# A two-layer hybrid transformer in fp32 on one core: the gate and the decay of the linear attention, and the ends of the first workspace layer, are computed by other engines and in another order

## The chip, the cores and the metric

The kernel runs on one core of a Trainium2 chip. The core has five engines that run side by side, each with its own queue of instructions in a fixed order: TensorE (PE, matrix products and transposes; PEld is its loading of weights), VectorE (DVE), ScalarE (ACT), GpSimd (POOL) and SyncE (SP), which here starts all the transfers. Engines wait for each other through semaphores. The metric is the device time of one execution in microseconds (us); lower is better.

## The reference

The input x has 4 sequences of 512 rows of 256 numbers, all fp32. Eight blocks follow one another, each added to x: latent attention with 16 heads, a small feed-forward block, cosine-similarity attention, the feed-forward block again, gated linear attention, a workspace layer, attention with LoRA adapters, and a workspace layer again. The gated linear attention and the end of a workspace round are what the change touches:

```python
# gated linear attention, for each sequence, 16 heads (dk = 8, dv = 16)
gk = jax.nn.log_sigmoid(x @ Wgk1 @ Wgk2 + bgk2) / 16
S  = S * jnp.exp(gt)[..., None] + kt[..., None] * vt[..., None, :]     # step over t
ot = jnp.einsum('bhk,bhkv->bhv', qt, S)
o  = o * jax.lax.rsqrt(jnp.mean(o * o, axis=-1, keepdims=True) + EPS) * norm_w
o  = o * (g * jax.nn.sigmoid(g))              # g = x @ Wg
out = o.reshape(b, t, vd) @ Wo

# workspace layer, two rounds; 16 slots gather from x, then x reads the slots
ws = _rms(ws + written, norm_post_w)
x_b = ctx @ out_proj_w.T + out_proj_b         # ctx: attention of x over the slots
x  = _rms(x + x_b, norm_post_w)
# after the two rounds the layer's result is added to the residual x
```

In the LoRA attention each sequence has its own adapted weights, W + A B, chosen by an index of the sequence.

## The kernel before

Rows lie on the 128 partitions: a sequence is 4 tiles of 128 rows (NI = 4), and the 256 columns are 2 halves (NC = 2). x stays on the chip for the whole kernel, in one buffer per sequence, and is loaded once and stored once. The stages follow one another: latent attention (0 to about 700 us, with the feed-forward steps of finished sequences woven in), cosine attention (to 1411), gated linear attention (to about 1605), the first workspace layer (to about 1732), LoRA attention (from 1750), the second workspace layer (to about 2204), and the store.

The order of work on PE is the order of the program text, since the whole emission runs inside a manual schedule for PE. Later stages reach into earlier ones by generators: a table called `woven` gives points (n, k) of a stage's loop at which the next step of another generator is emitted. The order on DVE, ACT, POOL and SP is chosen by the language's scheduler, which plays the program through a timeline of its own and takes what comes first in it; a block under `high_priority` is taken earlier. Buffers come from pools with a fixed number of copies, and an instruction that writes a buffer waits until its last reader is done.

**Gated linear attention.** `gla_load` and `gla_fold` (L753 to L769) load and prepare the weights; among them is the bias column `bg`, read by ACT. `gla_stage` has `prepare(b, part)` for a sequence's projections: "norm" is the layernorm of x into `xn`, with the last step, x times 1/deviation plus an offset, on ACT (L178 makes the offset on DVE, L180 is the ACT step); "turned" transposes `xn` on PE (L195) and copies the result to `own_xt` on ACT (L196); part 1 is the decay (L815 to L821), parts 2 to 4 are v, q and k. `run` then goes through 4 sequences and 4 blocks of each; a block has two pairs of `states`: PE spreads v over partitions (L857), DVE multiplies with k in PSUM (L858) and scans over time, twice 512 columns (L861), POOL multiplies with q (L866), and PE sums (L876, `reads`). `gate` (L838 to L845) makes the gate of a sequence: a Sigmoid on ACT from PSUM, a reload of ACT's table for logarithm and exponential, and a DVE product with the same PSUM tile. `output` (L892 to L907) normalises by heads: a scaling on DVE (L899), ACT (L900, L901), four operations on POOL (L903 to L906; for the last sequence on DVE), and a DVE product (L907).

The decay of a sequence is exp of log-sigmoid over 16, with log-sigmoid(z) = min(z, 0) − ln(1 + exp(−|z|)). Before, ACT makes z (L815), |z| (L816), exp (L817), ln (L818), DVE takes min and subtracts (L819), ACT takes the exponential (L821).

A generator `first` folds the gated stage's weights and prepares sequence 0 at the points (15, 0), (15, 1), (15, 3), (16, 1) and (16, 2) of the cosine stage, and, as its last step at (16, 3), the layernorm of sequence 1.

**Workspace layer.** `ws_load` (L962) loads its weights and scales some of them on DVE (L968, L970, L971). In `ws`, `layernorm` writes the normalised x to `xf` on ACT; `turned` transposes it. Each of two rounds picks and gathers rows for the slots, and then goes over the sequences, a few steps apart: `attend`, `turn`, and `read` (L1224 to L1243): PE multiplies, DVE adds to `xf` (L1228), ACT squares for the mean (L1231), DVE and ACT make 1/root (L142 to L148, L143 and L144), DVE multiplies by it and by the weight `post` (four times L1234), and in round 1 DVE adds the result to the residual x (L1243).

**LoRA attention.** `lora_steps` (L1325) makes for a sequence the layernorm (with the last step on DVE, L185), two adapted weights (`adapted`: a DVE scaling L1347, two pairs of PE products, a DVE addition L1352), the transposes (L1362) with an ACT copy (L1363), and projections with rotary products on DVE (L1375) and sums on POOL. For the first sequence all of it is emitted after the workspace layer's last instruction. `keep(n)` (L217) emits n products of the identity with a mask into a spare PSUM buffer.

## Time and profile before

| | us |
|---|---|
| median of 3 runs (2207.63 to 2209.11) | 2208.92 |
| the profiled execution | 2209.9 |
| its span, first to last instruction | 2208.2 |
| PE busy in the span | 1985.9 |
| DVE busy | 1301.7 |
| ACT busy | 764.2 |
| POOL busy | 562.1 |
| mean granted TensorE clock (1 is full) | 0.953 |

The time of an execution is longer than its span by what lies around the first and the last instruction, here 1.7 us. In a line of a timeline the first number is the start from the span's beginning, the second the duration, then the engine, the source line, the operation, the written and the read buffers, and the shapes (partitions by columns); "x8" is a run of eight like instructions, and the bracket gives the time that the engine stood idle just before and what ended it.

### The profile page before, as it was taken

Reading aid. Unit: us, or ns where it says so; the run is one execution under the profiler, and the core shown is the slowest. Engines: PE = TensorE matmul, PEld = TensorE weight load, DVE = VectorE, ACT = ScalarE, POOL = GpSimd, SP = SyncE. Lnnn points to the kernel's source line nnn. Section 1 sums busy time; section 2 is a strip of 40 time slices with the busy share of each in tenths; the row PEclk is TensorE's granted clock in tenths of the full one; section 3 lists DMA queues with packets and bytes.
Section 4 is the critical chain, followed back from the end, with each engine's and each line's share of the span. In section 5 each row is a group of like instructions: output and inputs, shape, how many; then the busy total and the mean of one; then the engine's idle time right before and its main releaser. Section 6 shows DMA issues by size and latency. Waiting matters only on the chain.

```text
span 2208.2 us, 25496 instructions
## 1 busy us (share of the span) xinstructions
PE 1985.9 (90%) x9348; PEld 1061.1 (48%) x9348; DVE 1301.7 (59%) x3225; ACT 764.2 (35%) x1696; POOL 562.1 (25%) x489
## 2 busy tenths in 40 slices
PE   6999999998899999999999999787787679998885
PEld 4556555564444544544455454433254434444454
DVE  4565655656446435644753554599945766667455
ACT  2433434434223222322232242243134224334442
POOL 2333333433212122112211222065510012222100
PEclk9999999999899999999999999898789889999898
DMA  4020000000000000000000000100000000000001
GB/s 173 1 89 1 1 1 1 1 1 1 20 0 0 1 0 0 1 0 0 1 1 1 0 0 1 45 0 0 1 24 1 0 1 1 1 1 1 1 1 39
DMA packets 19838, 22.88 MB, mean 10 GB/s; under 512 B 4832, under 2 KB 17664, under 8 KB 19328
## 3 DMA queue, kind: packets, MB, share of 16 engines
...
q8 instruction: 74, 1.21, 0.2%
...
## 4 chain that ended last, share of the span: by engine, by line
PE 60%; DVE 18%; issue 11%; ACT 5%; POOL 4%; DMA 1%; SPq 0%; POOLq 0%; DVEq 0%; ACTq 0%
PE ps_two L215 26%; PE ps_acc L215 10%; PE ps_two L366 6%; PE ps_two L1410 4%; PE ps_acc L405 3%; PE ps_two L393 3%; DVE ps_two L233 3%; POOL e L661 2%; DVE gs L861 2%; PE ps_two L1452 2%; DVE ln_st L166 1%; PE ps_acc L1196 1%; DVE ps_st L858 1%; PE ps_two L628 1%; DMA x<-in_x 1%
## 5 line engine op out<-in xcount | busy, mean ns | idle before, releaser
L661 POOL TENSOR_TENSOR e<-e 128x1024 f32<-128x1024 f32 x64 | 150.6, 2353 | 623.0 <-ACT e L653 604.7
L233 DVE CUSTOM_DVE_ANT_0 ps_two<-ps_two,mask 128x128 f32<-128x128 f32 (+3 forms) x512 | 249.7, 502 | 80.2 <-PE ps_two L366 43.6
L653 ACT ACTIVATE e<-ps_two 128x1024 f32<-128x1024 f32 x128 | 130.7, 1022 | 351.1 <-PE ps_two L215 350.9
L215 PE MATMUL ps_acc<-e,cv 128*128 128x512 f32 x512 | 235.0, 602 | 1.4 <-DVE cot L659 0.9
L215 PE MATMUL ps_two<-cq,ckt 128*128 128x512 f32 x512 | 232.1, 596 | 3.0 <-DVE cq L630 3.0
L378 POOL TENSOR_TENSOR prob<-prob,psum_row 128x256 f32<-128x256 f32 (+3 forms) x128 | 159.4, 1254 | 289.2 <-DVE psum_row L377 283.0
L373 ACT ACTIVATE prob<-ps_two,nmax 128x128 f32<-128x128 f32 (+3 forms) x256 | 132.3, 525 | 148.4 <-DVE nmax L233 137.6
L215 PEld LDWEIGHTS ps_acc<-e,cv 128*128 128x128 f32 x512 | 93.4, 190 | 138.6 <-issue 115.8
L215 PEld LDWEIGHTS ps_two<-cq,ckt 128*128 128x128 f32 x512 | 97.2, 191 | 117.9 <-issue 115.5
L215 PE MATMUL ps_two<-own_xt,s 128*128 128x512 f32 x200 | 108.0, 672 | 18.4 <-DVE prt L129 10.6
L215 PE MATMUL ps_two<-own_xt,s16a 128*128 128x512 f32 x256 | 114.9, 593 | 0.1
L215 PE MATMUL ps_two<-s16b,cot 128*128 128x256 f32 x512 | 113.1, 379 | 0.0
L366 PE MATMUL ps_two<-kvt,qx 64*128 64x384 f32 (+3 forms) x512 | 104.5, 485 | 8.8 <-ACT qx L354 4.7
L1441 ACT ACTIVATE lo_ex<-ps_two 128x1024 f32<-128x1024 f32 (+3 forms) x128 | 85.4, 704 | 73.8 <-PE ps_two L1410 69.5
L393 PE MATMUL ps_two<-ident,prob 128*128 128x128 f32 x640 | 96.1, 282 | 15.5 <-POOL prob L378 5.8
L393 PEld LDWEIGHTS ps_two<-ident,prob 128*128 128x128 f32 x640 | 72.1, 143 | 76.7 <-issue 49.1
L215 PEld LDWEIGHTS ps_two<-s16b,cot 128*128 128x128 f32 x512 | 97.3, 190 | 20.1 <-issue 7.7
L1442 POOL TENSOR_SCALAR_AFFINE_SELECT lo_ex<-lo_ex 128x256 f32<-128x256 f32 x128 | 51.5, 407 | 196.5 <-ACT lo_ex L1441 195.3
L662 DVE TENSOR_TENSOR es<-e 128x512 f32<-128x512 f32 x64 | 43.9, 686 | 95.1 <-POOL e L661 94.0
L366 PE MATMUL ps_two<-kpe,qy 64*128 64x384 f32 (+3 forms) x512 | 91.5, 434 | 1.1 <-POOL qy L300 1.1
L1410 PE MATMUL ps_two<-lo_qm,lo_t 32*128 32x128 f32 (+3 forms) x512 | 78.0, 488 | 10.0 <-ACT lo_ex L1441 5.3
L405 PE MATMUL ps_acc<-prt,kv 128*64 128x256 f32 (+3 forms) x512 | 80.1, 457 | 3.4 <-DVE prt L129 3.4
...
## 6 DMA issues: line engine op xcount, KB each, us to landing
...
```

Of the source, the lines that this page charges most:

```text
L215: self.nc.tensor.matmul(out, lhsT=l, rhs=r, start=k == 0, stop=k == n - 1)
L233: self.nc.vector.tensor_tensor_reduce(out=sc[:, :n], in0=sc[:, :n], in1=self.mask[:, T - n :], scale=-1.0, scalar=3.0e38, op0=ALU.add, op1 ...
L366: nc.tensor.matmul(sc[:, k, :n], lhsT=q[r, rows], rhs=key[r, :n], start=first, stop=not first)
L373: nc.scalar.activation(pr[:, k, :n], sc[:, k, :n], AF.Exp, bias=nm[:, k : k + 1], scale=-1.0, accum_out=sm[:, k : k + 1],)
L378: nc.gpsimd.tensor_tensor(pr[:, :, :n], pr[:, :, :n], sm.unsqueeze(2).to_broadcast([P, 2, n]), op=ALU.mult)
L393: nc.tensor.transpose(pt[:, k, keys], pr[:, k, keys], self.ident)
L405: nc.tensor.matmul(po[k * R : (k + 1) * R, j * P :], lhsT=s.kv[:, j, 0, :], rhs=prt[:, k, j, j * P :], start=j == 0, stop=j == NI - 1,)
L653: nc.scalar.activation(t.e[:, pair * 2 : pair * 2 + 2, :], sc, AF.Exp)
L661: nc.gpsimd.tensor_tensor(e2, t.e[:, 0:2, :], t.e[:, 2:4, :], op=ALU.add)
L1410: nc.tensor.matmul(scs[k // 2][:, k % 2, : keys], lhsT=left[r, rows], rhs=right[r], start=True, stop=True)
L1441: nc.scalar.activation(ex[:, hs, :], sc[:, :, :n], AF.Exp, scale=0.25)
L1442: nc.gpsimd.affine_select(out=ex[:, hs, :P], in_=ex[:, hs, :P], compare_op=ALU.is_ge, fill=0.0, base=0, pattern=[[0, 2], [1, P]], channel_ ...
```

## The change

Four places are edited.

1. The gate of the linear attention is one ACT function, Silu, from PSUM; the Sigmoid and the DVE product go. The decay is written with the opposite sign: ACT takes |z| and relu(−z) from PSUM, with the bias and the new column `nbg` = −bias, then exp and ln as before; the sum of the two, −log-sigmoid, is made by DVE for sequence 0 and by POOL for the others (it was DVE for all), and the last exponential has the factor −1/16. `nbg` is made by one more DVE instruction in `gla_fold`, which the scheduler puts into the latent attention's part of DVE's order, behind a StreamShuffle there and ahead of two masked maxima.
2. The layernorm of sequence 1 is emitted with high priority at (15, 3) of the cosine stage, right after part 1 of sequence 0; the step at (16, 3) goes. The four scalings of `ws_load` are POOL's.
3. In round 1 of a workspace layer `read` multiplies `xf` by `post` into a tile `xp` as soon as `xf` is there (in the first layer one shared buffer, in the second the buffer `xt[b]`), and later adds `xp` times 1/root to x in four DVE instructions; the separate addition goes. For b = 0 this has high priority.
4. The first LoRA sequence's two adapted weights, its layernorm (now with ACT's last step), six `keep` products and the transposes are emitted at (1, 1), (1, 2), (1, 4) and (1, 8) of the first workspace layer; some pools open earlier for that.

The order of the transfers on SP stays. On ACT the table loads stay, one before each gate and one after.

```diff
--- before.py
+++ after.py
@@ -762,6 +762,8 @@
         nc.vector.tensor_scalar_mul(w["wq"], w["wq"], 8.0 ** -0.5)
         for c in range(NC):
             nc.vector.tensor_scalar_mul(w["wo"][:, c, :], w["wo"][:, c, :], w["nw"][:, c : c + 1])
+        w["nbg"] = wp.tile([P, 1], F32, name="gla_nbg", tag="gla_nbg")
+        nc.vector.tensor_scalar_mul(w["nbg"], w["bg"], -1.0)
         w["wz"] = wp.tile([P, NC, P], F32, name="gla_wz", tag="gla_wz")
         for c in range(NC):
             pz = self.ps()
@@ -812,13 +814,13 @@
                 pz = self.ps()
                 proj(pz, w["wz"], s.xt)
                 z, az = tile("gz", 1), tile("gaz", 1)
-                nc.scalar.activation(z, pz, AF.Identity, bias=bg)
-                nc.scalar.activation(az, z, AF.Abs)
+                nc.scalar.activation(az, pz, AF.Abs, bias=bg)
+                nc.scalar.activation(z, pz, AF.Relu, bias=w["nbg"], scale=-1.0)
                 nc.scalar.activation(az, az, AF.Exp, scale=-1.0)
                 nc.scalar.activation(az, az, AF.Ln, bias=1.0)
-                nc.vector.scalar_tensor_tensor(z, z, 0.0, az, op0=ALU.min, op1=ALU.subtract)
+                (nc.vector if isinstance(place, list) else nc.gpsimd).tensor_tensor(z, z, az, op=ALU.add)
                 s.dec = tile("gdec", 1)
-                nc.scalar.activation(s.dec, z, AF.Exp, scale=1.0 / 16)
+                nc.scalar.activation(s.dec, z, AF.Exp, scale=-1.0 / 16)
             elif part == 2:
                 pv = self.two()
                 for c in range(NC):
@@ -840,9 +842,8 @@
                 for c in range(NC):
                     proj(pg[:, c, :], wg, s.xt, slice(c * P, (c + 1) * P))
                 s.g = p2.tile([P, NC, T], F32, name="gg", tag="gg")
-                nc.scalar.activation(s.g, pg, AF.Sigmoid)
+                nc.scalar.activation(s.g, pg, AF.Silu)
                 self.logs()
-                nc.vector.tensor_tensor(s.g, s.g, pg, op=ALU.mult)
 
             def states(b, n, pair):
 
@@ -965,10 +966,10 @@
         w |= {n: self.load_col(pool, f"ws_{n}") for n in ("pre", "cb", "bq", "bkv")}
         w["slots"] = self.load(pool, "ws_slots")
         for c in range(NC):
-            nc.vector.tensor_scalar_mul(w["cw"][:, c, :], w["cw"][:, c, :], w["pre"][:, c : c + 1])
-
-        nc.vector.tensor_tensor(w["slots"], w["slots"], w["wb"], op=ALU.add)
-        nc.vector.tensor_scalar_mul(w["ob"], w["ob"], 0.25)
+            nc.gpsimd.tensor_scalar_mul(w["cw"][:, c, :], w["cw"][:, c, :], w["pre"][:, c : c + 1])
+
+        nc.gpsimd.tensor_tensor(w["slots"], w["slots"], w["wb"], op=ALU.add)
+        nc.gpsimd.tensor_scalar_mul(w["ob"], w["ob"], 0.25)
         return w
 
     def ws_fold(self, w, pool, once):
@@ -1022,7 +1023,7 @@
         for h in range(4):
             m, rows = h % 2, slice(h * 32, h * 32 + 32)
             nc.vector.tensor_tensor(w["ob"][rows], w["ob"][rows], pb[rows, m, :D], op=ALU.add)
-    def ws(self, w, order):
+    def ws(self, w, order, woven={}):
 
         nc, S, R = self.nc, 16, P
         with self.pool("ws_1", 1) as p1, self.pool("ws_2", 2) as p2:
@@ -1222,25 +1223,46 @@
                 nc.scalar.copy(atts[b], pt)
 
             def read(b, vo, rnd):
+
+                if rnd == 1 and b == 0:
+                    with self.tc.high_priority(offset=2000):
+                        reading(b, vo, rnd)
+                else:
+                    reading(b, vo, rnd)
+
+            def reading(b, vo, rnd):
                 py = self.two().rearrange("p a (i d) -> p (a i) d", d=D)
                 for i in range(NI):
                     self.mm(py[:, i, :], [(atts[b][:, i * P : (i + 1) * P], vo[:, b // 2, :])])
                 nc.vector.tensor_tensor(xf[b], xf[b], py, op=ALU.add)
+                if rnd == 1:
+
+                    if woven:
+
+                        xp = p2.tile([P, NI, D], F32, name="ws_xp", tag="ws_xp", bufs=1)
+                    else:
+                        xp = xt[b].rearrange("p c t -> p (c t)").rearrange("p (i d) -> p i d", d=D)
+                    nc.vector.tensor_tensor(
+                        xp, xf[b], w["post"].unsqueeze(1).to_broadcast([P, NI, D]), op=ALU.mult
+                    )
                 for i in range(NI):
                     junk = p2.tile([P, D], F32, name="ws_junk2", tag="ws_junk2")
                     nc.scalar.activation(junk, xf[b][:, i, :], AF.Square, accum_out=rms[:, b, i : i + 1])
                 self.rpow(rms[:, b, :], rms[:, b, :], 1.0 / D, 1e-6, self.tmps())
+                if rnd == 1:
+                    for i in range(NI):
+                        nc.vector.scalar_tensor_tensor(
+                            self.x[b][:, i, :], xp[:, i, :], rms[:, b, i : i + 1], self.x[b][:, i, :],
+                            op0=ALU.mult, op1=ALU.add,
+                        )
+                    return
                 for i in range(NI):
                     nc.vector.scalar_tensor_tensor(
                         xf[b][:, i, :], xf[b][:, i, :], rms[:, b, i : i + 1], w["post"], op0=ALU.mult, op1=ALU.mult
                     )
-                    if rnd == 0:
-                        junk = p2.tile([P, D], F32, name="ws_junk2", tag="ws_junk2")
-                        nc.scalar.activation(junk, xf[b][:, i, :], AF.Square, accum_out=ms[:, i, b : b + 1])
-                if rnd == 0:
-                    self.rpow(ms[:, :, b], ms[:, :, b], 1.0 / D, 1e-6, self.tmps(), wide[:, :, b])
-                if rnd == 1:
-                    nc.vector.tensor_tensor(self.x[b], self.x[b], xf[b], op=ALU.add)
+                    junk = p2.tile([P, D], F32, name="ws_junk2", tag="ws_junk2")
+                    nc.scalar.activation(junk, xf[b][:, i, :], AF.Square, accum_out=ms[:, i, b : b + 1])
+                self.rpow(ms[:, :, b], ms[:, :, b], 1.0 / D, 1e-6, self.tmps(), wide[:, :, b])
 
             if True:
                 for b in range(B):
@@ -1270,6 +1292,8 @@
                             if n > 5:
                                 self.keep(2)
                             turned(n - 5)
+                        if (rnd, n) in woven:
+                            next(woven[rnd, n], None)
 
 
 
@@ -1296,11 +1320,6 @@
         nc.vector.tensor_scalar(lm, cnt, 3.0, w["lidx"], op0=ALU.min, op1=ALU.is_equal)
         return w
 
-    def lora(self, w, tiles):
-        with self.pool("lora_2", 2) as p2:
-            for _ in self.lora_steps(w, range(B), tiles, p2):
-                pass
-
     def lora_tiles(self, p1):
 
         nc, ONE = self.nc, self.ONE
@@ -1322,7 +1341,8 @@
             nmt.append(t)
         return wide, vv, nmt
 
-    def lora_steps(self, w, order, tiles, p2):
+    def lora_stage(self, w, order, tiles, wpool):
+
 
 
 
@@ -1343,25 +1363,25 @@
 
         def adapted(s, n):
 
-            am = p2.tile([P, D], F32, name=f"lo_am{n}", tag=f"lo_am{n}", bufs=1)
+            am = wpool.tile([P, D], F32, name=f"lo_am{n}", tag=f"lo_am{n}", bufs=1)
             nc.vector.tensor_scalar_mul(am, w[f"a{n}"], lm[:, s.b : s.b + 1])
             pw = self.two()
             for c in range(NC):
                 self.mm(pw[:, c, :], [(am[:, c * P : (c + 1) * P], w[f"b{n}"])])
-            wb = p2.tile([P, NC, 512], F32, name=f"lo_w{n}b", tag=f"lo_w{n}b")
+            wb = wpool.tile([P, NC, 512], F32, name=f"lo_w{n}b", tag=f"lo_w{n}b")
             nc.vector.tensor_tensor(wb, w[f"w{n}"], pw, op=ALU.add)
             return wb
 
         def norm(s):
             xn, s.xt = self.norm_tiles()
             self.layernorm(xn, self.x[s.b])
-            s.wqk = adapted(s, "qk")
+            if s is not seqs[0]:
+                s.wqk = adapted(s, "qk")
             pt = self.two()
             for c in range(NC):
                 for i in range(NI):
                     nc.tensor.transpose(pt[:, c, i * P : (i + 1) * P], xn[:, i, c * P : (c + 1) * P], self.ident)
             nc.scalar.copy(s.xt, pt)
-            s.qk = p2.tile([P, 2, G, T], F32, name="lo_t", tag="lo_t")
 
         def project(s, i):
             cols = slice(i * P, (i + 1) * P)
@@ -1397,6 +1417,8 @@
             elif part == 1:
                 s.wvo = adapted(s, "vo")
             elif part < 7:
+                if part == 2:
+                    s.qk = p2.tile([P, 2, G, T], F32, name="lo_t", tag="lo_t")
                 if part < 6:
                     project(s, part - 2)
                 if part > 2:
@@ -1488,37 +1510,55 @@
                     )
                 nc.vector.tensor_tensor(self.x[s.b], self.x[s.b], py, op=ALU.add)
 
-        for part in range(7):
-            prepare(seqs[0], part)
+        p2 = None
+
+        def first():
+            s = seqs[0]
+            s.wqk = adapted(s, "qk")
             yield
-        for m in range(NI):
-            maxima(*todo[0], m)
+            s.wvo = adapted(s, "vo")
             yield
-        lowered(*todo[0])
-        at = (2, 5, 6, 7, 8, 9, 10)
-        for n in range(len(todo) + 2):
-            s, g = todo[n] if n < len(todo) else (None, None)
-            nxt = todo[n + 1] if n + 1 < len(todo) else None
-            prev = todo[n - 1] if 0 < n <= len(todo) else None
-            last = todo[n - 2] if n > 1 else None
+            xn, s.xt = self.norm_tiles()
+            with self.tc.high_priority(offset=2000):
+                self.layernorm(xn, self.x[s.b], True)
+            yield
+            self.keep(6)
+            self.turned(xn, s.xt)
+            yield
+
+        def run(pool):
+            nonlocal p2
+            p2 = pool
+            for part in range(2, 7):
+                prepare(seqs[0], part)
+            for m in range(NI):
...
+        return first, run
 
     def store(self):
         for b in range(B):
@@ -1562,13 +1602,14 @@
                     place = shared("s16a")
                     for part in (0, 1, 3, 4, 2):
                         prepare(0, part, place)
+                        if part == 1:
+                            with m.tc.high_priority(offset=2000):
+                                prepare(1, "norm", None)
                         if part != 3:
                             yield
-                    prepare(1, "norm", None)
-                    yield
 
                 g = first()
-                woven |= {at: g for at in ((15, 0), (15, 1), (15, 3), (16, 1), (16, 2), (16, 3))}
+                woven |= {at: g for at in ((15, 0), (15, 1), (15, 3), (16, 1), (16, 2))}
                 m.cos(cos, woven)
             wp = ctx.enter_context(pool("late_w", side="right"))
             ws = m.ws_load(wp)
@@ -1579,12 +1620,13 @@
                 extra = {n: [ffn[B - 1]] for n in (1, 3, 5)} | {n: [fold] for n in (6, 9, 10, 13, 14, 15)}
                 run(range(B), extra, g2, g3)
         lora = m.lora_load(wp, [shared("s8"), shared("s4a"), shared("s4b")])
-        with pool("lora_1", side="right") as l1:
-            tiles = m.lora_tiles(l1)
+        with pool("lora_1", side="right") as l1, pool("lora_w", 2) as lw, m.norms("norm_2", xn=1, xt=2):
+            first, run = m.lora_stage(lora, range(B), m.lora_tiles(l1), lw)
             with m.psum("ps_2", two=2, acc=4):
-                m.ws(ws, ("by", "xt", "xf"))
-            with m.psum("ps_3", two=4), m.norms("norm_2", xn=1, xt=2):
-                m.lora(lora, tiles)
+                g = first()
+                m.ws(ws, ("by", "xt", "xf"), {(1, n): g for n in (1, 2, 4, 8)})
+            with m.psum("ps_3", two=4), pool("lora_2", 2) as l2:
+                run(l2)
         with m.psum("ps_4", two=2, acc=4):
             m.ws(ws, ("xf", "xt", "by"))
         m.store()
```

## The prediction

> **What bounds the kernel now.** I read the page's totals and slices first, then the busy times by stretch, then the timelines of the engines around the edited lines. TensorE (PE) is busy 90% of the span and carries 60% of the chain that ended last; the third line is the clock that was granted.
>
> ```profile
> PE 1985.9 (90%) x9348; PEld 1061.1 (48%) x9348; DVE 1301.7 (59%) x3225; ACT 764.2 (35%) x1696; POOL 562.1 (25%) x489
> ...
> DVE  4565655656446435644753554599945766667455
> ...
> PEclk9999999999899999999999999898789889999898
> ...
> PE 60%; DVE 18%; issue 11%; ACT 5%; POOL 4%; DMA 1%; SPq 0%; POOLq 0%; DVEq 0%; ACTq 0%
> ```
>
> The 90% is a mean. VectorE (DVE) reads 9 in three slices, and PE's clock dips just there. By stretch (length, busy time of PE, weight load, DVE, ScalarE (ACT), GpSimd (POOL), granted clock, DMA):
>
> ```profile
> 1330.00:1400.00 70.00, 69.63 (x237) 34.93 (x239) 29.14 (x31) 18.17 (x22) 14.11 (x6) 1.00 0.00 0
> 1400.00:1480.00 80.00, 63.31 (x216) 27.78 (x214) 66.58 (x123) 29.36 (x47) 30.38 (x14) 0.85 0.12 31
> 1480.00:1600.00 120.00, 91.06 (x346) 34.88 (x340) 114.49 (x146) 35.14 (x58) 65.43 (x38) 0.82 0.00 1
> 1600.00:1700.00 100.00, 79.86 (x432) 50.49 (x432) 52.81 (x153) 41.18 (x138) 9.64 (x15) 0.91 0.05 14
> ```
>
> In the cosine stage (before 1411 us) PE is full and ACT is three quarters idle. In the gated stage (1411 to 1605) DVE is full: 114.49 of 120 us. There a DVE instruction less is time less. The start of the stage, PE and then DVE:
>
> ```profile
> 1412.74 1.13 PE L857 MATMUL ps_st<-s16a,s4b 32*128 32x512 f32 x4 [1.36 <-issue]
> 1426.56 2.80 PE L195 MATMUL ps_two<-ident,xn 128*128 128x128 f32 x8 [12.69 <-ACT xn L180]
> ```
>
> ```profile
> 1425.73 0.14 DVE L178 SCALAR_TENSOR_TENSOR ln_off<-ln_mv,ln_rstd 128x4 f32<-128x4 f32 x1
> ...
> 1426.60 1.86 DVE L971 TENSOR_SCALAR r_ws_ob<-r_ws_ob 128x256 f32<-128x256 f32 x1
> ...
> 1438.71 1.22 DVE L845 TENSOR_TENSOR gg<-gg,ps_two 128x1024 f32<-128x1024 f32 x1 [2.31 <-ACT gg L843]
> ...
> 1444.47 1.94 DVE L819 SCALAR_TENSOR_TENSOR gz<-gz,gaz 128x512 f32<-128x512 f32 x1
> ```
>
> PE stands 12.69 us for sequence 1's normalised rows (xn), because their offset L178 queues on DVE behind other work; then the second state pair follows. L971, L845, L819 are lines the change takes off DVE.
>
> **The change, part by part** (gains positive, against the profiled execution: 2209.9 us, span 2208.2 plus 1.7 around it, 1.0 above the median 2208.92).
>
> A, the new negated bias. One DVE instruction joins the MLA stage after the StreamShuffle that ends at 153.0, and waits for the load of gla_bg: issued at 148.92, 5.7 to landing, so 154.6. Queued behind it are the masked maxima that began at 152.90; for these wait ACT's exponentials and PE's transposes. DVE starts them 1.7 late; DVE then has pauses of 1.87 and 1.43, PE is nearly full. I take −0.9, between 0 (pauses absorb it) and −2.0 (all shifts).
>
> B, the start of the gated stage. Sequence 1's layernorm (8 statistics instructions, 5 small DVE ones, 2+4 on ACT; no DMA) goes into the cosine stage; its DVE and ACT time lies beside PE there (29.14 and 18.17 of 70 us; cost at most 0.5 if a copy for PE waits behind the 2.07 us of L180; taken as 0). The eight transposes then follow the first states at about 1414, not 1426.56. DVE also loses L971 1.86, L968 0.38, L970 0.42, L845 1.22 with the wait of 2.31, and L819 1.94. Laying the order anew with these durations (a pair is L858 1.21 and two scans 2.33), both first pairs are scanned by 1427.7, before 1436.4; the fifth L858 comes at 1440.4, not 1448.57: +8.2. What is late next is ACT's copy of own_xt, behind four small functions. Bounds 6 (that copy or the gate's PSUM buffer holds PE's next projection, 6.32 us) to 9.
>
> GpSimd gets the four workspace scalings. No row shows them there; by its 128x512 rows (0.61 one input, 1.27 two) they are 0.2 to 0.7 each, about 1.5 in all. Its pause after the first product was 8.24, so they cost nothing while it lasts; else at most 1.5, inside B's lower bound. The first stands ahead of the first product and waits for a load that landed at 1425.2 and whose buffer now comes free about 2.6 earlier.
>
> C, the rest of the stage. Off DVE go three L845 (1.21 each) and two L819 (2.20, 2.56), 8.4 in all; on GpSimd come three adds of 128x512 at 1.27. Silu takes Sigmoid's place (1.02, with its two table loads of 1.28 as before; I take Silu at that same duration), Abs and Relu that of Identity and Abs. Sequence 1 returns about 1.1, since PE's states come next at 1471.4; sequence 2 about 1.8, as L907 waits for GpSimd's L903 to L906, which the add pushes back by 1.27; sequence 3 about 1.1. Sum +4, bounds 0 (L907 and the hold below take all) to 8.4.
>
> ```profile
> L819 DVE SCALAR_TENSOR_TENSOR gz<-gz,gaz x3: 1940/2196/2562, 1444.5 to 1530.3; 128x512 f32<-128x512 f32 x3
> ...
> L819 DVE SCALAR_TENSOR_TENSOR s16a<-s16a x1: 627/627/627, 1399.5 to 1399.5; 128x512 f32<-128x512 f32 x1
> ```
>
> L819 takes 0.63 alone and 1.94 to 2.56 beside GpSimd's products; so does an L145 of four columns (2.35 at 1490.05, beside a product from 1490.04 of 2.34, against 0.16 elsewhere). In places DVE stands until GpSimd is done, and what this hold took from L819 can fall on the next instruction: the reason for half of 8.4. The Trainium skill's "GPSIMD Engine Reference", section 8 (Key points), says that GpSimd shares SBUF interfaces with VectorE and meets instructions there that read two SBUF inputs. The rows agree, and read strictly it speaks against the move: three adds would hold DVE up to 3.8 us, and the sum would be 11.5 instead of 15.3.
>
> D, gated stage to workspace. ACT's L180 for the first two sequences ran at 1602.07 to 1606.10, while DVE waited for a load; in the new order they stand behind L900, L901 and the last small functions, together with the third (three times 2.07 from about 1615). Two DVE scalings of the LoRA adapter (0.33 each) come into the same stretch. L1072 begins at about 1631.5, not 1630.56: −1.0; bounds 0 and −2.5 (one set of L180 and an adapter scaling late).
>
> E, workspace end to LoRA.
>
> ```profile
> 1728.35 3.62 PE L215 MATMUL ps_two<-ws_vo,ws_att 128*128 128x256 f32 x16
> 1750.25 3.75 PE L215 MATMUL ps_two<-s4a,lo_amqk 128*128 128x512 f32 x4 [18.28 <-issue]
> ```
>
> PE idles 18.28 us while DVE works without a gap: four residuals, four layernorms. The change puts two adapter products (1.88 each, as at 1754.80) before PE's last reads, which end 3.6 later, at about 1735.6. From the last L1228 (1732.00) to the first rope product (1759.38) DVE had 26.3 us of work. Of it 4.6 goes: two L1352 (2.3), four L1347 (1.0), the four L185 of sequence 0 (1.3, now ACT); 0.9 fits into pauses of 0.49 and 1.48 between the reads. 1735.6+26.3−4.6−0.9 = 1756.4: +3.0. The early transposes, cold at 2.80, a copy of 1.01 and a projection of up to 3.75 are done by then. What follows has the same order, so the gain stays. Bounds 1 (the two L1352 delay the reads too) to 5 (PE's products fall into its own pauses).
>
> F, end of the second workspace layer. The products with the post weight fill the same pauses and the separate residual add goes (L1243 1.22, but the product costs as much): the last x update ends at 2201.9 instead of 2203.94: +2.0, bounds 1 and 2.3. The store after it is unchanged.
>
> Sum: −0.9+8.2+4+0−1.0+3.0+2.0 = +15.3. 2209.9 − 15.3 = 2194.6, and on the median 2193.6; I say 2194. All lower bounds together give +3.5, all upper ones +24.7.
>
> **The rivals.** (1) The middle gives nothing. If L907 and the hold eat C and D costs 2.5, the sum is 9.8: 2199. For it: L907 waits for GpSimd in two of four cases; against: DVE is at 95%.
>
> (2) All DVE time counts: B 9, C 8.4, E 4.5, F 2.3, less 1.9 is 22.3: 2186.6. For it: the full DVE; against: PE's order is fixed and its states gate DVE in sequence 1.
>
> (3) The moved layernorm does not free PE: transposes still at 1426.56, as something else (the PSUM buffer) holds them. The third pair then waits for PE's projection at 1431.29 to 1437.6, B falls to 3.2, the sum to 10.3: 2198.6. Against: the profile names only xn.
>
> (4) Slower, by the clock. The mean granted clock is 0.953 over 1985.9 us of PE; a hundredth less costs 20.8. To undo 15.3 and lose 4.4 more it must fall by 0.0095 over the whole span; a fall of 0.0105 costs 21.8 and gives 2216.4 on the execution, 2215.4 on the median. For it: 0.82 where DVE binds; against: the dips stand where PE idles, which the change shortens, and three runs agree within 1.5 us.
>
> A second rule weighs on Silu. "ScalarE: Activation LUTs", What ACT_TABLE_LOAD costs, gives a switch 1283 ns and a drain of 1380, about 2.66. The trace shows 1.28 for L843's load. If Silu's set took one more switch for each of four gates, an estimate from that page is 10.6, and the sum would be 4.7 instead of 15.3; the order of instructions keeps one load before each gate and one after.
>
> **How the numbers follow.** Forecast (2189 to 2198) 0.52; rival 1 0.21; rival 2 0.13; rival 3 0.05; rival 4, or another loss above 20 us, 0.09. This measurement tells 0.2%, 4.4 us, from no change: faster is below 2204.5. Of rival 1 a fifth lies above that: 0.04; the rest of it and of the others, 0.87, is faster; slower 0.09. The range takes the bounds' sums less their least likely ends: 2185 to 2205.
>
> **What would show it.** In the profile after: transposes of xn near 1414 without 12.69 us before them (B); the gated stage 11 to 13 us shorter with DVE still full; L907 waits for GpSimd (C); 18.28 replaced by a wait near 14, 20.8 us, not 27.4, from the start of the fourth L1228 to the first rope product (E); a pause of under 2 us near 153 (A). Wrong would make it: a Silu longer than 1.02, a table load more, more idle before L907, or a lower clock in the first 1300 us, which the change hardly touches.

## The result: 2198.66 us, 0.5% faster, where 2194 had been forecast

The changed kernel takes 2198.66 us (median of 6 executions, 2196.63 to 2201.26) against 2209.12 us for the kernel before (6 executions, 2207.63 to 2209.60). The ratio is 0.9954 with a 95% interval of 0.9942 to 0.9965. The sign was right and the time lies in the range; the gain is 10.5 us where 15.3 was the sum. The profiled execution took 2196.69 us, its span is 2194.6 us, 13.6 us less than before.

### The profile after

The totals, the busy tenths of VectorE (DVE), the granted clock and the chain that ended last, of the kernel after:

```profile
PE 1992.2 (91%) x9360; PEld 1062.1 (48%) x9360; DVE 1294.0 (59%) x3212; ACT 764.8 (35%) x1700; POOL 569.4 (26%) x496
...
DVE  4565655756446435644754454598945766667455
...
PEclk9999999999999999999999999988789889999898
...
PE 59%; DVE 19%; issue 11%; ACT 5%; POOL 4%; DMA 2%; SPq 0%; POOLq 0%; DVEq 0%; ACTq 0%
```

In the page one of DVE's three 9s has become an 8, and DVE has 7.7 us less to do in all. The same stretches as before (start and end, length, busy time of PE, weight load, DVE, ACT and POOL, granted clock, DMA):

```profile
1330.00:1400.00 70.00, 69.63 (x238) 35.16 (x231) 29.72 (x30) 19.32 (x26) 14.12 (x6) 1.00 0.00 0
1400.00:1480.00 80.00, 67.33 (x231) 28.38 (x229) 69.04 (x108) 30.34 (x51) 41.78 (x24) 0.89 0.12 31
1480.00:1600.00 120.00, 94.63 (x344) 36.99 (x344) 105.22 (x138) 32.41 (x49) 60.29 (x32) 0.79 0.01 3
1600.00:1700.00 100.00, 77.18 (x426) 49.12 (x426) 51.19 (x160) 40.50 (x140) 9.07 (x17) 0.88 0.03 11
```

POOL's time between 1400 and 1480 goes from 30.38 to 41.78. The work that came to it, three scaling rows (0.85, 0.70 and 0.72) and two sums (1.26 and 1.28), makes 4.8 of these 11.4; the rest is the stage's own work, which now falls earlier. DVE is still the fullest engine between 1480 and 1600, though that stretch now also holds a little of the next stage's start.

### Where the 13.6 us came from

To see the stages apart, each DVE instruction of the kernel before was matched with the same one after, and the time by which it starts earlier was read at eight places: 1300 us (inside the cosine stage, all code up to there being the same but for the new negated bias), the last instructions of the cosine stage (1404), the start of the fifth state pair (1448), the scaling L899 of the last sequence (1604.5), the last pick of the workspace layer (1704.9), the first rope product (1759.4), the end of the LoRA attention (2186) and the end of the span. The differences between neighbouring places are the gain of each stage. Gains in us, by the profiled execution; "rest" is the sum without the first column:

| kernel | to 1300 | cosine end | B: start of gated | C: rest of gated | D: workspace | E: end, to LoRA | LoRA | F: last end | rest | span |
|---|---|---|---|---|---|---|---|---|---|---|
| predicted | -0.9 | 0 | 8.2 | 4.0 | -1.0 | 3.0 | 0 | 2.0 | 16.2 | 15.3 |
| after | 3.9 | -0.6 | 5.5 | 3.4 | -4.5 | 2.2 | 1.4 | 2.4 | 9.7 | 13.6 |
| after, run again | 2.5 | -0.6 | 5.9 | 3.4 | -4.5 | 2.2 | 1.4 | 2.4 | 10.2 | 12.7 |
| part 1 alone | 3.4 | 0.0 | 3.2 | 4.7 | -0.2 | 0.0 | 0.0 | -0.1 | 7.6 | 11.1 |
| sequence 1's layernorm moved alone | 4.5 | -0.6 | 3.4 | 1.2 | -0.9 | -0.9 | -1.3 | -0.3 | 0.7 | 5.2 |
| part 3 alone | 8.0 | 0.0 | 0.6 | -2.6 | -0.2 | 0.5 | 2.4 | 2.4 | 3.1 | 11.1 |
| part 4 alone | 9.3 | 0.0 | 0.5 | -2.6 | -3.6 | 2.9 | 0.4 | 0.0 | -2.3 | 7.0 |
| after without part 4 | 3.9 | -0.6 | 6.1 | 3.2 | -0.7 | 0.3 | -1.0 | 2.3 | 9.8 | 13.6 |
| ws_load scalings back on DVE | 3.6 | -0.6 | 4.0 | 1.5 | -4.4 | 2.2 | -1.7 | 2.4 | 3.4 | 7.0 |
| adapter scalings on GpSimd | 2.0 | -0.6 | 5.5 | 3.4 | -3.7 | 2.6 | -5.8 | 2.4 | 3.8 | 5.8 |
| adapter scalings on ScalarE | 5.0 | -0.6 | 5.5 | 3.5 | -0.3 | 2.2 | 0.7 | 2.4 | 13.4 | 18.4 |
| that, and products in place of keep | 6.9 | -0.6 | 5.3 | 3.8 | -1.6 | 5.8 | -1.6 | 2.4 | 13.6 | 20.5 |
| the same, run again | 8.0 | -0.6 | 5.3 | 3.8 | -1.6 | 5.8 | -1.5 | 2.4 | 13.6 | 21.6 |
| ws_fold copies on ScalarE | 7.9 | -0.6 | 5.5 | 3.6 | -4.4 | 2.2 | -1.5 | 2.4 | 7.2 | 15.2 |

Three things are read from it. The first column is up to 9.3 us in code that the change hardly touches: most of it goes with the clock (below) and not with the change. The rest comes to 9.7 to 10.2 us in the two profiles of the kernel after, not 16.2. And of the missing 6, B lost about 2.5 and D about 3.5.

The other columns are not free of the clock either. Parts 3 and 4 alone show -2.6 in C, whose code neither of them touches; 1.7 of it comes at one place, where the eight products of a gate take 6.43 and 6.45 us at a granted clock of 0.57, against 5.32 at 0.69 in the kernel before, and DVE waits for them. In the LoRA attention (1759 to 2186 us) the profile before has 15 half-speed windows of the clock; 13 of them go with +2.4 (part 3 alone), 14 with +1.4 (after), 16 with -1.7 (scalings back on DVE) and 17 with -5.8 (adapter scalings on GpSimd), though the two profiles with products in place of keep have 13 and show -1.6 and -1.5. So two us in one column are the price of an edit only where the rows show it.

### The profile page after: what moved, and what is told of

Its sections match the earlier page's. It is cut to its first block, busy times and chain, and to the rows that moved or that the text cites. A ratio compares the mean times of both kernels' runs of the same rounds, so it can differ in the third digit from the quotient of the medians.

```text
span 2194.6 us, 25518 instructions
## 1 busy us (share of the span) xinstructions
PE 1992.2 (91%) x9360; PEld 1062.1 (48%) x9360; DVE 1294.0 (59%) x3212; ACT 764.8 (35%) x1700; POOL 569.4 (26%) x496
## 3 DMA queue, kind: packets, MB, share of 16 engines
q8 instruction: 74, 1.21, 0.2%
## 4 chain that ended last, share of the span: by engine, by line
PE 59%; DVE 19%; issue 11%; ACT 5%; POOL 4%; DMA 2%; SPq 0%; POOLq 0%; DVEq 0%; ACTq 0%
PE ps_two L215 25%; PE ps_acc L215 10%; PE ps_two L366 5%; PE ps_two L1432 3%; PE ps_acc L405 3%; DVE ps_two L233 3%; PE ps_two L393 3%; DVE gs L862 2%; POOL e L661 2%; PE ps_two L1474 2%; DVE ln_st L166 1%; PE ps_acc L1197 1%; DVE ps_st L859 1%; DMA x<-in_x 1%; PE ps_two L628 1%
## 6 DMA issues: line engine op xcount, KB each, us to landing
s16a<-in_mla_wqn SPq DMA_DIRECT2D x1, 1536.0 KB, 11.4
```

## The experiments

Each short diff is against the kernel before for the four single parts, and against the kernel after for all others. The line numbers in the profile's rows are each kernel's own: in the kernel after, the state pair's product is L859, the scans are L862, GpSimd's product L867, the last read's addition L1237, the adapter scaling L1367, the adapted weight L1372, the rope product L1395.

### One part at a time

Part 1 alone (the gate and the decay):

```diff
-                nc.scalar.activation(s.g, pg, AF.Sigmoid)
+                nc.scalar.activation(s.g, pg, AF.Silu)
                 self.logs()
-                nc.vector.tensor_tensor(s.g, s.g, pg, op=ALU.mult)
...
-                nc.vector.scalar_tensor_tensor(z, z, 0.0, az, op0=ALU.min, op1=ALU.subtract)
+                (nc.vector if isinstance(place, list) else nc.gpsimd).tensor_tensor(z, z, az, op=ALU.add)
```

> The first part of the change alone: Silu, the decay by Abs and Relu with the negated bias, the add on GpSimd for sequences 1 to 3. Theory after the comparison of the two profiles: at the start of the gated stage VectorE loses L845 with its wait and L819, but TensorE still waits for sequence 1's rows until 1426.6 and the third pair then waits for TensorE: 3.2 us; the middle gives 3.3 as in the profile after; the negated bias costs 0.2. Sum 6.3, about 2202.8. Rival: without the moved layernorm the start gives nothing, only the middle does: 3, about 2206. A second rival, GpSimd's adds hold VectorE: 0 or slower, 2209.

Measured: 2198.14 us, ratio 0.9950 (0.9938 to 0.9963). By stage B is 3.2 and C is 4.7, and only 0.3 of it is lost up to the end. The start of the gated stage on PE in this kernel:

```profile
1423.10 2.81 PE L195 MATMUL ps_two<-ident,xn 128*128 128x128 f32 x8 [12.69 <-ACT xn L180]
```

The wait of 12.69 us for the normalised rows is there unchanged, and B is 3.2: the number that rival (3) gave for a start of the stage in which the layernorm does not free PE.

Sequence 1's layernorm moved into the cosine stage, and nothing else:

```diff
+                        if part == 1:
+                            with m.tc.high_priority(offset=2000):
+                                prepare(1, "norm", None)
                         if part != 3:
                             yield
-                    prepare(1, "norm", None)
-                    yield
```

> The second part without the scalings: only sequence 1's layernorm goes into the cosine stage. Theory: the transposes come at about 1414 and the first two pairs are scanned together, but VectorE keeps L971, L968, L970, L845 and L819, so the fifth pair comes 2 to 4 us earlier: about 2206. Rival, the idle time of 12.69 us is what bounds: 6 or more, 2203 or less. Second rival, the pause of VectorE only moves to the gate (L845 waits longer for ScalarE): 0 to 1, 2208.5.

Measured: 2206.30 us, ratio 0.9992 (0.9983 to 1.0001). It costs 0.59 us in the cosine stage; every kernel with this move shows 0.58 or 0.59 there and every kernel without it at most 0.02. It gains 3.4 in B and 1.2 in C, and with the 0.6 and what the later stages lose, 0.7 us are left at the end.

Part 3 alone (the early product with the post weight):

```diff
+                if rnd == 1:
+                    ...
+                    nc.vector.tensor_tensor(
+                        xp, xf[b], w["post"].unsqueeze(1).to_broadcast([P, NI, D]), op=ALU.mult
+                    )
...
-                if rnd == 1:
-                    nc.vector.tensor_tensor(self.x[b], self.x[b], xf[b], op=ALU.add)
```

> The third part alone: round 1's product with the post weight early, one instruction fewer at the end, in both workspace layers. Theory: 2.4 at the end of the second layer as the profile after shows, and about 1.5 of the same kind at the end of the first, which carries on into the LoRA stage: 3.9, about 2205. Rival: the first layer's end is hidden behind the LoRA weights, so 2 to 2.4 only: 2206.8.

Measured: 2200.38 us, ratio 0.9970 (0.9958 to 0.9982). By stage it is 3.1: 0.5 up to the first rope product, 2.4 in the LoRA attention, whose code is the same and which has two half-speed windows fewer than before, and 2.4 at the end of the second workspace layer, less 2.2 in stages that it does not touch, C above all. F is 2.3 or 2.4 in all ten profiles that have this part, and between -0.3 and 0 in the three that have not. That is the clearest gain of the change.

Part 4 alone (the first LoRA sequence emitted inside the workspace layer):

```diff
+                        if (rnd, n) in woven:
+                            next(woven[rnd, n], None)
...
+                m.ws(ws, ("by", "xt", "xf"), {(1, n): g for n in (1, 2, 4, 8)})
```

> The fourth part alone: the first LoRA sequence's adapted weights, layernorm and transposes in the first workspace layer. Theory after the comparison: the two adapter scalings go ahead of the last sequence's normalisation on VectorE (one of them took 2.04 us) and the three sets of L180 behind it on ScalarE; 3 to 4.5 us are lost between the gated stage and the workspace layer, and about 3 gained at the LoRA stage's start: 2209 to 2210.5, not faster. Rival, as recorded: 1.0 lost and 2 to 3 gained: 2207 to 2208.

Measured: 2207.59 us, ratio 0.9994 (0.9985 to 1.0003). It loses 3.6 in D and gains 2.9 in E: no gain on balance. The four medians, taken each from that of before on the same chip, would add up to some 21 us (10.3, 2.1, 8.1 and 0.8), twice what the change brings, although the scalings of ws_load are in none of the four. By stage, without the first column, they add up to 9.1, and to 10.6 with the 1.5 that the scalings are worth in B (below), against 9.7 to 10.2 for the whole. The medians carry something that does not belong to the edits.

### The change again, and the change without its fourth part

> The changed kernel once more, beside the variants below on one chip. Theory: the four parts add up by stage to about 10 (gate 7.6 less the part shared with the layernorm, end of the layers 3 to 4, LoRA part 0), so 2198 to 2199 with the kernel before at 2208.4 to 2209. Rival: the parts alone added to 20 because they do, and the first six runs of the changed kernel were unlucky in where TensorE's clock dips fell: then about 2190 to 2194.

The same code as the kernel after: 2195.77 us, ratio 0.9941 (0.9929 to 0.9952). All stages behind the first column repeat within 0.4 us.

> The change without its fourth part (the first LoRA sequence stays where it was). Theory: the two adapter scalings and the late L180 cost 3 to 4.5 between the gated stage and the workspace layer, and the early weights give back about 3: leaving the part out costs nothing, 2197 to 2199. Rival, as recorded (1.0 lost, 3.0 gained, 0.9 of it by the third part): about 1.5 slower than the changed kernel, 2200 to 2201.

The kernel after with the functions of the LoRA attention and their calls as before: 2196.38 us, ratio 0.9945 (0.9932 to 0.9958). D goes from -4.5 to -0.7, E from 2.2 to 0.3, and the rest is 9.8 as in the kernel after. So part 4, as it is emitted, is worth nothing in these profiles, and D's loss comes and goes with it (some 2 us of that go with the clock, as shown next).

### What is D? The adapter scalings on two other engines

At the end of the gated stage, DVE and GpSimd in the kernel after (start, length, engine, line, operation):

```profile
1595.44 0.69 DVE L904 TENSOR_TENSOR grp<-grp,grs 128x512 f32<-128x512 f32 x1
1596.04 2.04 DVE L1367 TENSOR_SCALAR lo_amqk<-s4a,lo_lm 128x256 f32<-128x256 f32 x1
1598.00 0.33 DVE L1367 TENSOR_SCALAR lo_amvo<-s4a,lo_lm 128x256 f32<-128x256 f32 x1
1598.26 0.68 DVE L905 TENSOR_TENSOR grp<-grp,grs 128x512 f32<-128x512 f32 x1
1598.86 1.21 DVE L952 TENSOR_TENSOR x<-x,ps_two 128x1024 f32<-128x1024 f32 x1
```

```profile
1596.13 1.80 POOL L1335 MEMSET lo_v<- 128x2048 f32 x1 [8.27 <-PE ps_two L215]
```

The first scaling takes 2.04 us, the second, of the same shape, 0.33. The first ends with GpSimd's memset, at 1598.1 and 1597.9: such an instruction, which lasts until one of GpSimd's is done, is called held here. Both stand ahead of the residual L952 of the third sequence, for which its layernorm, ACT's L180 and PE wait. In the kernel without part 4 the same addition starts 3.14 us earlier, of which 0.44 was there before the two scalings:

```profile
1595.72 1.22 DVE L952 TENSOR_TENSOR x<-x,ps_two 128x1024 f32<-128x1024 f32 x1 [0.28 <-PE ps_two L215]
```

Two kernels take the scalings off DVE, the first to GpSimd, the second to ScalarE (ACT).

```diff
-            nc.vector.tensor_scalar_mul(am, w[f"a{n}"], lm[:, s.b : s.b + 1])
+            (nc.gpsimd if s is seqs[0] else nc.vector).tensor_scalar_mul(am, w[f"a{n}"], lm[:, s.b : s.b + 1])
```

> The changed kernel with the first LoRA sequence's two adapter scalings on GpSimd. In the profile after, the first of them took 2.04 us beside GpSimd's memset of 1.80 that began 0.09 later. Theory of the hold: the next VectorE instruction (L905) is held by the memset instead, so 0.3 to 0.7 is gained, not 2.3, and L905 is seen at about 2 us. Rival: the scalings were the loss, and 2.3 us come back before the last residual of the gated stage.

Measured: 2202.71 us, ratio 0.9973 (0.9962 to 0.9984). D is still -3.7, since GpSimd's work now falls on another instruction of DVE. DVE, and GpSimd, of this kernel:

```profile
1599.88 2.67 DVE L906 TENSOR_SCALAR grp<-grp 128x512 f32<-128x512 f32 x1
```

```profile
1597.45 1.28 POOL L1367 TENSOR_SCALAR lo_amqk<-s4a,lo_lm 128x256 f32<-128x256 f32 x1 [12.72 <-DVE lo_lm L1320]
1598.71 0.92 POOL L1367 TENSOR_SCALAR lo_amvo<-s4a,lo_lm 128x256 f32<-128x256 f32 x1
1599.58 0.95 POOL L1330 MEMSET lo_wide<- 128x1024 f32 x1
1600.47 1.80 POOL L1335 MEMSET lo_v<- 128x2048 f32 x1
```

L906 took 0.41 in the kernel after; here it lasts until 1602.55, beside the two memsets, the second of which ends at 1602.27. The 5.8 us that this kernel loses in the LoRA attention, whose code is that of the kernel after, go with the clock: there are 17 half-speed windows there and 14 in the kernel after, the granted clock is 0.933 against 0.944, and PE is busy for 373 us against 368. So this median does not show that the edit itself is slower.

```diff
+            if s is seqs[0]:
+                nc.scalar.activation(am, w[f"a{n}"], AF.Copy, scale=lm[:, s.b : s.b + 1])
+            else:
+                nc.vector.tensor_scalar_mul(am, w[f"a{n}"], lm[:, s.b : s.b + 1])
```

> The changed kernel with the two adapter scalings of the first LoRA sequence on ScalarE, which is idle there for 9 us. They were the 2.37 us on VectorE ahead of the third sequence's residual; on GpSimd they moved the hold to L906 (2.67 us). Theory of the hold: GpSimd's memset of 1.80 holds L906 or its neighbour again, and from the last L900 to the second round of the workspace layer 3.5 to 4.5 are lost as before. Rival: the scalings themselves were the loss, and this stretch loses 2.1 or less, 2.4 better.

Measured: 2192.62 us, ratio 0.9934 (0.9917 to 0.9950). D is -0.3. DVE and GpSimd of this kernel in the same place:

```profile
1595.54 1.22 DVE L952 TENSOR_TENSOR x<-x,ps_two 128x1024 f32<-128x1024 f32 x1
1596.67 0.42 DVE L906 TENSOR_SCALAR grp<-grp 128x512 f32<-128x512 f32 x1
```

```profile
1594.77 1.81 POOL L1335 MEMSET lo_v<- 128x2048 f32 x1 [8.17 <-PE ps_two L215]
```

The memset is as long as before, but it runs from 1594.77 to 1596.58 and L906 begins just behind it; beside it stand L905 (0.69), which reads two tiles in SBUF, and L952, which takes 1.21 or 1.22 elsewhere too. A hold that simply moves to the next instruction, as it did with the scalings on GpSimd, was not seen here.

Of the 4.2 us between -4.5 and -0.3, 2.1 are there when DVE has passed this place. The other 2.1 come later, at two groups of PE's products, first in the kernel after, then with the scalings on ScalarE:

```profile
1603.85 6.51 PE L215 MATMUL ps_two<-s,go 128*128 128x256 f32 x16 [4.41 <-DVE rp L142]
1695.24 2.07 PE L215 MATMUL ps_acc<-w_ws_ww,ws_gt 128*128 128x256 f32 x4 [0.46 <-ACT ws_gt L1121]
```

```profile
1600.54 5.38 PE L215 MATMUL ps_two<-s,go 128*128 128x256 f32 x16 [2.46 <-DVE rp L142]
1690.70 1.13 PE L215 MATMUL ps_acc<-w_ws_ww,ws_gt 128*128 128x256 f32 x4 [0.46 <-ACT ws_gt L1121]
```

The granted clock was 0.56 and 0.50 in the first pair and 0.68 and 1.00 in the second; in the kernel before the same groups took 5.14 and 1.13. So half of the 4.2 us is the price of the two scalings on DVE in that place, and half goes with the clock. Whether the later arrival, with its longer pause of PE (4.41 against 2.46), brought the slow windows there was not separated.

### What is missing in B? The held copies

The start of the gated stage, on PE, DVE and GpSimd in the kernel after:

```profile
1409.46 1.13 PE L858 MATMUL ps_st<-s16a,s4b 32*128 32x512 f32 x4 [1.36 <-issue]
1410.52 1.09 PE L195 MATMUL ps_two<-ident,xn 128*128 128x128 f32 x8
```

```profile
1424.71 2.36 DVE L985 COPY ws_bv<-c_ws_bkv 128x64 f32<-128x64 f32 x1
1426.99 0.81 DVE L142 TENSOR_SCALAR rp<-ln_mv 128x4 f32<-128x4 f32 x2
...
1434.35 1.94 DVE L1318 TENSOR_SCALAR lo_cnt<-lo_cnt 128x4 f32<-128x4 f32 x1
```

```profile
1424.68 2.34 POOL L867 TENSOR_TENSOR gqs<-gs,s16a 128x1024 f32<-128x1024 f32 x1
...
1433.88 2.39 POOL L867 TENSOR_TENSOR gqs<-gs,s16a 128x1024 f32<-128x1024 f32 x1 [6.18 <-DVE lo_le L1316]
```

The transposes follow the first states at once, at 1410.52, as predicted. But a copy of 64 columns takes 2.36 us beside a product on GpSimd from 1424.68 to 1427.02, and a scaling of 4 columns takes 1.94 beside the next. In the kernel before these two stood where GpSimd was idle, after its product of 1425.96 to 1428.31:

```profile
1425.96 2.35 POOL L866 TENSOR_TENSOR gqs<-gs,s16a 128x1024 f32<-128x1024 f32 x1 [39.41 <-DVE ln_off L178]
```

```profile
1429.09 0.18 DVE L984 COPY ws_bv<-c_ws_bkv 128x64 f32<-128x64 f32 x1
...
1432.74 0.17 DVE L1294 TENSOR_SCALAR lo_cnt<-lo_cnt 128x4 f32<-128x4 f32 x1
```

A third, the first of the two L142 (0.74, elsewhere 0.16), stands beside one of the scalings that came to GpSimd (L971 there, 0.72 from 1426.98). The excess, 2.18, 1.77 and 0.58, is more than the 2.7 us that B lacks. One kernel takes the copies away from DVE, another puts the four scalings of ws_load back on it.

```diff
-        nc.vector.tensor_copy(bias[:, :, 0], w["bq"])
-        nc.vector.tensor_copy(bias[:, :, 1], w["bkv"][:, :NC])
+        nc.scalar.copy(bias[:, :, 0], w["bq"])
+        nc.scalar.copy(bias[:, :, 1], w["bkv"][:, :NC])
...
-        nc.vector.tensor_copy(bv, w["bkv"][:, NC:].unsqueeze(2).to_broadcast([P, NC, 32]))
+        nc.scalar.copy(bv, w["bkv"][:, NC:].unsqueeze(2).to_broadcast([P, NC, 32]))
```

> The changed kernel with the three small copies of the workspace fold (L982 to L985) on ScalarE. In the profile after, L985 took 2.36 us on VectorE and ended with GpSimd's second product. Theory of the hold: the next small instruction (L142) is held until the product ends, and the fifth pair of the gated stage comes at the same time within 0.4. Rival: the copy itself was slow, and the fifth pair comes 2.2 earlier.

Measured: 2196.18 us, ratio 0.9952 (0.9940 to 0.9965). B is 5.5, as in the kernel after. With the copies gone, the next small instructions on DVE are held, the first L142 (2.40) by the same product on GpSimd, the second (0.77) by the scaling behind it:

```profile
1420.76 3.09 DVE L142 TENSOR_SCALAR rp<-ln_mv 128x4 f32<-128x4 f32 x2
```

```profile
1420.78 2.35 POOL L867 TENSOR_TENSOR gqs<-gs,s16a 128x1024 f32<-128x1024 f32 x1
```

Here the hold does move on, and B gains nothing by it. The rival, that the copy itself was slow, is excluded.

```diff
-            nc.gpsimd.tensor_scalar_mul(w["cw"][:, c, :], w["cw"][:, c, :], w["pre"][:, c : c + 1])
+            nc.vector.tensor_scalar_mul(w["cw"][:, c, :], w["cw"][:, c, :], w["pre"][:, c : c + 1])
...
-        nc.gpsimd.tensor_tensor(w["slots"], w["slots"], w["wb"], op=ALU.add)
-        nc.gpsimd.tensor_scalar_mul(w["ob"], w["ob"], 0.25)
+        nc.vector.tensor_tensor(w["slots"], w["slots"], w["wb"], op=ALU.add)
+        nc.vector.tensor_scalar_mul(w["ob"], w["ob"], 0.25)
```

> The changed kernel with the four workspace scalings back on VectorE. Theory of the hold: the small instructions after the scans (L985 2.36, L142 0.81) were held by GpSimd's product in the scalings' place, so the fifth pair comes at most 0.8 later than in the changed kernel: no difference that can be measured. Rival: VectorE's 2.66 us of scalings come back in full, and the kernel is 2.5 slower.

Measured: 2201.69 us, ratio 0.9964 (0.9951 to 0.9977). B is 4.0 and C 1.5, where the kernel after has 5.5 and 3.4. DVE of this kernel:

```profile
1424.72 2.01 DVE L972 TENSOR_SCALAR r_ws_ob<-r_ws_ob 128x256 f32<-128x256 f32 x1
...
1434.31 2.56 DVE L1316 TENSOR_SCALAR lo_le<-lo_stf 128x4 f32<-128x4 f32 x4
```

The scaling L972 catches a product's hold now, and the last of four comparisons of 4 columns (0.36 for the four in the kernel after) that of the next. So the move of the scalings to GpSimd is worth 1.5 us in B, between the 0.8 of the theory and the 2.5 of the rival, although an instruction of DVE is held either way. The 1.9 that C lacks come with the clock: the eight products of a gate take 6.09 us at a granted clock of 0.60 here and 3.70 at 1.00 in the kernel after, and DVE waits for PE behind them. PE and DVE here, then PE in the kernel after:

```profile
1457.96 6.09 PE L215 MATMUL ps_two<-own_xt,s 128*128 128x512 f32 x8
```

```profile
1466.16 1.23 DVE L859 TENSOR_TENSOR ps_st<-ps_st,gqk 128x1024 f32<-128x1024 f32 x1 [3.14 <-PE ps_st L858]
```

```profile
1455.21 3.70 PE L215 MATMUL ps_two<-own_xt,s 128*128 128x512 f32 x8
```

### What limits E? The place of the adapter products

PE at the end of the first workspace layer in the kernel after, then the fourth addition to `xf` and the first rope product on DVE:

```profile
1724.73 3.62 PE L215 MATMUL ps_two<-ws_vo,ws_att 128*128 128x256 f32 x16
1728.18 5.31 PE L221 MATMUL ps_acc<-mask,ident 128*128 128x512 f32 x12
1740.13 2.81 PE L195 MATMUL ps_two<-ident,xn 128*128 128x128 f32 x8 [6.64 <-ACT xn L180]
1744.05 3.78 PE L215 MATMUL ps_two<-lo_wqkb,xt 128*128 128x512 f32 x4 [1.10 <-ACT xt L196]
```

```profile
1728.38 1.22 DVE L1237 TENSOR_TENSOR ws_xf<-ws_xf,ps_two 128x1024 f32<-128x1024 f32 x1
...
1749.57 0.69 DVE L1395 TENSOR_TENSOR lo_r<-ps_two,w_rope_c 128x512 f32<-128x512 f32 x1 [0.31 <-PE ps_two L215]
```

The 18.28 us without work on PE have become 11.8 us between the reads and the transposes, 5.31 of them `keep` products, and from the fourth addition to the first rope product it is 21.2 us, where 27.4 were and 20.8 were expected. But the two adapter products before the reads (1711.26 and 1715.30) make those 4.0 us later. The last variant emits these products in the place of two calls of `keep` in the same round, where PE only multiplies the identity with a mask; it builds on the version with the scalings on ScalarE.

```diff
-                self.keep(3)
+                if not first and woven:
+                    next(woven[1, "picked"], None)
+                else:
+                    self.keep(3)
...
-                self.keep(2)
+                if rnd == 1 and woven:
+                    next(woven[1, "written"], None)
+                else:
+                    self.keep(2)
...
-                m.ws(ws, ("by", "xt", "xf"), {(1, n): g for n in (1, 2, 4, 8)})
+                m.ws(ws, ("by", "xt", "xf"), {(1, n): g for n in ("picked", "written", 4, 8)})
```

> The same with the two adapter products (1.88 each) in the places of two keep calls of the second round (after the pick, and ahead of the last transposes of the slots) and not between the attention products. Theory: TensorE's last reads come 3.2 us earlier against the start of the round than in the changed kernel, since the products fall into waits for VectorE; the residuals and layernorms behind them follow, and the LoRA stage starts 2 to 3 earlier: about 2 us faster than the changed kernel. Rival: the two additions L1372 land in VectorE's serial chain of the pick, each 1.14, and eat what is gained: no difference.

Measured: 2190.60 us, ratio 0.9929 (0.9915 to 0.9943). PE of this kernel, one adapter product and the first two reads:

```profile
1690.90 1.88 PE L215 MATMUL ps_two<-s4b,lo_amvo 128*128 128x512 f32 x4
...
1709.54 1.89 PE L215 MATMUL ps_two<-ws_vo,ws_att 128*128 128x256 f32 x8
```

E rises to 5.8. D is 1.2 lower than with the scalings on ScalarE alone, because DVE's addition of an adapted weight (L1381 in this kernel, 1.20) now stands in the chain of the pick. Together D and E are 4.3, against 1.9 with the scalings on ScalarE alone, -2.3 in the kernel after and -0.3 without part 4: placed like this, part 4 is worth 4.6 us up to the start of the LoRA attention, in these profiles.

> The same code as the version with the adapter scalings on ScalarE and the adapter products in place of two keep calls, run once more. It asks two things. Whether the gain over before holds: median 2186 to 2194, ratio to before 0.990 to 0.994. And whether the latent attention's time (to 1300 us) belongs to the program or to the execution. Theory that it is the phase of the clock's half-speed windows against the work, new in each execution: the shift at 1300 differs from the first run's 6.9 us by one window or more (1.7 us each, so anything from 2 to 9.5), while the stages after it repeat within 1 us (start of the gated stage +5.3, first rope +5.8, end +2.4). Rival, that it belongs to the program: 6.9 within 0.5 again.

The same code once more: 2199.36 us, ratio 0.9963 (0.9951 to 0.9976). The two intervals, of one and the same code, do not touch; the runs were on two chips, on which the kernel before has medians of 2208.21 and 2208.02. The profiled executions agree to 1.1 us: 2187.7 and 2186.7 of span, every stage behind the first column within 0.1, the same count of half-speed windows, and 1.05 us of the 1.1 come from the first 45 us. For this pair the rival comes nearer, though 8.0 is not within 0.5 of 6.9: behind the first 45 us the first column is the same. It does not belong to the program alone, since the two profiles of the kernel after differ there by 1.4 (0.65 of it early), with 9 and 10 windows. And the six timed executions of this run went from 2188.36 to 2203.32, and they go with the mean granted clock: 0.960 for the fastest (the profiled one), 0.958 for 2195.24, 0.955 and 0.956 for 2199.23 to 2200.88, 0.954 for the slowest. All twelve executions of this code have a median of 2194.35, all eleven of the kernel after 2197.14. By stages this version is 3.3 to 3.9 us better than the kernel after, in two profiles of each; whether it is faster in an average execution is left open, since the intervals of the one code (0.9915 to 0.9943, 0.9951 to 0.9976) lie on both sides of those of the other (0.9942 to 0.9965, 0.9929 to 0.9952).

## Why the prediction came out as it did

The forecast of 2194, faster with 0.87, was right in sign; the time, 2198.66, is 4.7 above it. It is next to the 2198.6 of rival (3) and the 2199 of rival (1), neither of which describes what happened. The mechanism held in B's order, C, E and F; two sizes, B and D, were wrong.

**A, the new negated bias: right in place, too large.** The row after, on DVE, with the wait for the load:

```profile
153.34 0.15 DVE L766 TENSOR_SCALAR gla_nbg<-s4b 128x1 f32<-128x1 f32 x1 [1.41 <-DMA s4b<-in_gla_bg]
```

The wait is 1.41, as "a pause of under 2 us near 153" had it. At 160 us 0.2 of it was left; in the ten profiles that have the instruction it was 0 to 0.7, since the pauses behind it took the rest. The step took -0.9 and should have stood near its upper bound, 0.

**B, the start of the gated stage: the order right, a term missing.** The transposes came at once, and part 1 alone, without the moved layernorm, gave the 3.2 of rival (3). The fifth pair starts at 1439.78, near the 1440.4 of the prediction, but 3.3 us of this were there before the stage began, so B is 5.5 to 5.9 and not 8.2, a little under its lower bound of 6. The step that failed is "Laying the order anew with these durations": small DVE instructions were counted at 0.16 to 0.18, and GpSimd stretches three of them by 4.5 in all. It also took L971 (1.86) and L819 (1.94) off at full length, though both stood beside GpSimd's products: a scaling of L971's shape takes 0.33 alone (L1367 in the kernel after) and L819 takes 0.63, so that 2.8 of these 3.8 us were hold and not DVE's work. The same hold was used for C, with its row, and not looked for in B, into whose order the change brought GpSimd's first products. The scalings took GpSimd 2.27 us, not "about 1.5". That the missing 2.7 us are this hold less some slack is a reading of the rows; the run that took the copies away shows only that the hold then strikes the next instruction, and no run removed it.

**The moved layernorm in the cosine stage.** It was put at "at most 0.5", taken as 0; it costs 0.59, in all kernels alike.

**C, the rest of the gated stage: right in size.** 3.4 of 4.0, within 0 to 8.4. Of the 8.4 us taken off DVE two fifths came through. B and C together shorten the stage by 8.9 us, where "11 to 13 us shorter" was the sign. The wait for GpSimd before the gated product grew in the second sequence from 0.90 to 2.87, by more than the 1.27 of the added sum, and did not grow in the third. The row before and the row after:

```profile
1540.86 3.35 DVE L907 TENSOR_TENSOR go<-go,grs 128x1024 f32<-128x1024 f32 x1 [0.90 <-POOL grs L906]
```

```profile
1527.73 3.36 DVE L908 TENSOR_TENSOR go<-go,grs 128x1024 f32<-128x1024 f32 x1 [2.87 <-POOL grs L907]
```

The product itself takes 3.35 in the second and third sequences of both kernels, and 1.2 in the first, so that hold was in the trace of before. The gate's Silu takes 1.02 us and its table load 1.28, as assumed.

**D, gated stage to workspace: the worst step.** -1.0 was taken and -2.5 was the bound. At the first product with the gather weights (L1072) 8.7 us of 12.1 were left, so -3.4; another 0.3 and 0.8 go up to the last pick, which makes the -4.5 of the table. The prediction counted the two adapter scalings at 0.33 each and named ACT's L180 as what is late next. That term was mis-sized: the first scaling is held for 2.04, and the two cost 2.1 us where they stand, ahead of the third sequence's residual. With them on ScalarE the loss is 0.3, although the three sets of L180 run together in both (12 instructions in 5.99 us from 1604.17 in the kernel after, in 6.00 from 1600.86 there). Another 1.4 (16 products in 6.51 us, 5.14 before) and 0.9 (four in 2.07, 1.13 before) are half-speed windows of the clock, for which D had no term. The order that the scheduler chose puts the scaling ahead of the residual, and that was there to be read.

**E, workspace end to LoRA: right.** 2.2 of 3.0 in 1 to 5; 21.2 us to the first rope product against 20.8; the reads 4.0 later against 3.6; 11.8 us of PE between reads and transposes, where a wait near 14 was the sign. "What follows has the same order, so the gain stays" was not enough: the LoRA attention gained or lost between -5.8 and +2.4 with nearly the same code in it, mostly as the number of half-speed windows there went.

**F, end of the second workspace layer: right.** 2.4 of 2.0; the bound was 2.3.

**The rivals.** (1) expected that C gives nothing and D costs 2.5; C paid and D cost more, so its 2199 was right by its sum and not by its reasons. (2) is excluded: not all DVE time counts. (3) is excluded for the whole change and is what part 1 alone does. (4) named the clock as the danger, and the clock was of help in the profiled execution: the first 1300 us gave 3.9 us that no step of the sum contains. Without them the profiled execution would have taken about 2200.6 us, so a part of the agreement with the forecast is luck. A strict reading of the Trainium skill's "GPSIMD Engine Reference", section 8 (Key points), by which GpSimd meets DVE instructions with two SBUF inputs, gave a sum of 11.5, and the stages without the first column make 9.7 to 10.2. The held instructions here include a copy and scalings, which read one tile. The same sentence of the page also names DVE instructions in "a 2-port perf mode"; the prediction left that half out, and whether these ran in such a mode no run here shows.
